# First experts and edge windows stepped beside the attention's node tiles

## The chip, the cores and the metric

The kernel runs on one core of one Trainium2 chip. The metric is the device time of one execution in microseconds (us): the median of three timed runs, and beside them one execution recorded by the hardware profiler. An execution with the profiler on can take longer than a timed one; the table below has both.

Engines in the profile: PE is TensorE's matmul, PEld its weight load, DVE is VectorE, ACT is ScalarE, POOL is GpSimd, SP is SyncE, which here only issues DMAs.

## The reference

The reference is four layers over a graph of 3125 nodes with 256 features and 53125 edges sorted by their destination. Each layer adds a graph step and a feed-forward step to `x`. Only the first two steps and the preparation of the later layers touch the change.

```python
def gnn0(x, bias, src, dst):             # attention over each node's incoming edges, 8 heads of 32
    h = layernorm(x)
    q, k, v = h @ Wq.T / SCALING, h @ Wk.T, h @ Wv.T
    attn = einsum('ehd,ehd->eh', k[src], q[dst]) + bias
    a = exp(attn - segment_max(attn, dst)[dst])
    a = a / segment_sum(a, dst)[dst]
    return segment_sum(v[src] * a[:, :, None], dst) @ Wo.T

def ffn0(x):                              # a shared network, and the best 2 of 4 small experts
    h = layernorm(x)
    shared = relu(relu(h @ sW1 + b) @ sW2 + b) @ sW3 + b        # 256 -> 256 -> 128 -> 256
    out[e] = relu(relu(h @ eW1[e] + b) @ eW2[e] + b) @ eW3[e]   # 256 -> 128 -> 64 -> 256
    topw = softmax(top_k(softmax(h @ gW + gb), 2))
    return shared + sum(topw * out[chosen])

x = x + gnn0(x); x = x + ffn0(x)          # then layers 1 to 3, whose graph steps sum the
                                          # features of each node's neighbours
```

## The kernel before

**Tiles and stages.** The nodes are 25 tiles of 125 (`T`, `P`), and `x` stays on the chip. `attention()` (L1526) is the first graph step; then `experts0` (L750) is the first feed-forward step, and beside it `blocks` (L1858) prepares for the later layers, whose neighbour sums are matmuls with blocks of counts: for each pair of node tiles, how many edges lead from each node of the one to each of the other. After both come `convolutions`, `experts1` and the rest.

**What sets the order.** A scheduling layer puts each engine's instructions in the order in which the Python code issues them and adds the waits. A tile taken from a pool waits until the last reader of the buffer has finished, so `bufs` says how far an engine may run ahead. Generators that one function runs with `next` place the work of another in between. The queues of SP and POOL issue DMAs in order.

**The attention's loop.** Its setup writes keys and values of all nodes to `kv_d` in DRAM, and finds `first`, the index of each node tile's first edge. Each tile has 18 columns of 128 edges (`WC`), in three parts of six (`PC`). Per tile, in the order of the loop at L1809:

- `logits` (three parts): POOL gathers six times 128 rows of `kv_d` (L1559, buffers `kv`, seven of them); PE multiplies a turned one-hot with the queries, held as three bf16 parts, into `qx` (L1738, three PSUM banks, a bank for two columns and six matmuls); DVE multiplies keys with it (L1741) and sums over each head (L1742).
- `sums_of`: adds the edges' bias, an Exp on ACT (L1751), and 18 matmuls that add up per node (L1754), read into `sums` (L1756).
- `weights_of`, for the tile before: 18 matmuls bring each node's shift back to its edges (L1766), DVE subtracts (L1767), ACT takes the Exp (L1771).
- `weighted`, for the tile before: DVE weighs the values (L1776), ACT casts the one-hot (L1781), and 18 matmuls in float32 of 265 columns collect `acc` (L1783, two PSUM banks).
- `one_hot`, `one_hot_turned`, `queries`, for the tile after: one-hots, 18 transposes (L1724), the loads `lt_t` (L1702) and `eb_t` (L1704) on SP, and the query product.
- `normed`, `normed_turned`, `projected`, for the tile before: division by the sum of weights, two transposes (L1800), the product with `wo`, and the addition to `x` (L1807). `normed` also writes the tile's in-degrees to `deg`.

The small products share the PSUM name `sm` (three banks).

**The first experts.** `experts0` goes by seven groups of four or three tiles (`GROUPS`), 500 or 375 columns, with pools of two buffers. A group is a layer norm (a Sqrt on ACT), eight transposes into `lt`, `gates` (some 25 small operations on DVE and an Exp on ACT), seven hidden products (`product` at L233, each followed by `relu_into`, which takes DVE at L745 and ACT at L747 in turn), the gates' spread over the experts (L809), and per tile a product `po` that is added to `x` (L817). Weights lie in one slot `wslot`, loaded by SP. After each of nine products a group calls `next(beside)`, one step of `blocks`.

**The count blocks.** `blocks` first finds, for each group of five nodes (`GN`; 25 groups to a tile, 625 in all), where its edges begin: prefix sums of `deg` as three matmuls and a scan, a store of `ptr_d` and a load of `win_at` on SP. Ten gathers on POOL (L1907) fetch the 128 edges from there on, sources and destinations; they are transposed (L1913) and turned by DVE operations on 625 columns into the row and tile of the source and the place of the destination (`row_h`, `til_h`, `col_h`). Then, for each of 25 destination tiles: three comparisons on DVE (L262: `hr`, `hc`, `hs`), 25 pairs of matmuls (L1960, L1962) whose results leave by DVE or ACT (L197, L199) as `ab`, 25 transposes (L1972) into `an`, and the stores of `ab` to `at_d` and of `an` to `an_d` (L105 and L106, two DMAs each on SP). From the third on, every second tile also issues one of ten clears of `xs_d`.

```python
attention()
with weights("main"):
    ...
        steps = blocks(bp, bps)
        experts0(steps)
        for _ in steps:
            pass
```

Of the kernel before, what the change touches and what calls it, by code (L numbers as in the profile page):

```python
# [26 lines left out]
E = 53125  # L27
# [14 lines left out]

GN = 5
# [25 lines left out]
def gnn_ffn_kernel(ctx: ExitStack, tc: tile.TileContext, a, out: bass.AP):  # L69
# [4 lines left out]
    wpools = []  # L74
# [42 lines left out]
    @contextmanager  # L117
    def weights(name):

        with tc.tile_pool(name="w" + name, bufs=2, reuse_waits="tile") as p:  # L120
            wpools.append(p)
            yield
            wpools.pop()

    def slot():
        return wpools[-1].tile([128, SLOT], F32, name="wslot", tag="wslot")
# [13 lines left out]
    def bias_rows(*names):  # L140


        v = wpools[-1].tile([3, ROWS], F32, name="wbias_in", tag="wbias_in", bufs=1)
        h = wpools[-1].tile([3, ROWS], BF16, name="wbias_h", tag="wbias_h", bufs=1)
        t = wpools[-1].tile([3, ROWS], BF16, name="wbias", tag="wbias")
# [20 lines left out]
    class Packer:  # L166
# [5 lines left out]
        def put(self, ap, rows_, shape):  # L172
            n = 1
            for s in shape:
                n *= s
            v = self.t[:rows_, self.at:self.at + n]
            if len(shape) == 2:
                v = v.rearrange("p (a b) -> p a b", a=shape[0])
            elif len(shape) == 3:
                v = v.rearrange("p (a b c) -> p a b c", a=shape[0], b=shape[1])  # L180
            nc.sync.dma_start(v, ap)
            self.at += n
            assert self.at <= SLOT
            return v
# [565 lines left out]
    def experts0(beside=iter(())):  # L750
# [17 lines left out]
        with ExitStack() as es:  # L768
            pool = es.enter_context(tc.tile_pool(name="ex0", bufs=2, reuse_waits="tile"))
            psum = es.enter_context(tc.tile_pool(name="ps_ex0", bufs=2, space=PSUM, reuse_waits="tile"))  # L770

            pick = pool.tile([4, 2, 128], F32, name="pick", bufs=1)
            nc.vector.tensor_copy(pick.rearrange("e p (j c) -> e (p j) c", j=2),
                                  ident[:4, :4].unsqueeze(2).to_broadcast([4, 4, 64]))
            for t0, n in GROUPS:
                ln = pool.tile([P, 4, D], F32, name="ln")
                normalize(pool, ln, x[:, t0:t0 + n, :], n, "a")
                lt = pool.tile([128, 2, 4, P], F32, name="lt")
                transposed(psum, lt, ln, n)
                g = gates(pool, psum, lt, n, gw, gb, 4, "softmax")  # L780
                gt = turned_gates(pool, psum, g, n, 4)
                c = n * P

                def hidden(name, m, terms, bias):
                    ps = psum.tile([128, 512], F32, name="tr")
                    product(ps[:m, :c], terms)
                    relu_into(name, ps[:m, :c], bias)
                    next(beside, None)

                s1 = pool.tile([128, 2, 4 * P], F32, name="s1")  # L790
                s2 = pool.tile([128, 4 * P], F32, name="s2")
                for m in range(2):
                    hidden(s1[:, m, :c], 128, [(sw1[:, k, m * 128:(m + 1) * 128], fan(lt[:, k, :n, :]))
                                               for k in range(2)], cols[:, m:m + 1])
                hidden(s2[:, :c], 128, [(sw2[:, k, :], s1[:, k, :c]) for k in range(2)], cols[:, 2:3])

                e2 = pool.tile([128, 2, 4 * P], F32, name="e2")
                for p in range(2):
                    ps2 = psum.tile([128, 512], F32, name="pair", bufs=1)
                    for j in range(2):  # L800
                        e = 2 * p + j
                        e1 = pool.tile([128, 4 * P], F32, name="e1")
                        hidden(e1[:, :c], 128, [(ew1[:, e, k, :], fan(lt[:, k, :n, :])) for k in range(2)],
                               cols[:, 3 + e:4 + e])
                        product(ps2[j * 64:(j + 1) * 64, :c], [(ew2[:, e, :], e1[:, :c])])
                    relu_into(e2[:, p, :c], ps2[:, :c], cols2[:, p:p + 1])
                    ps = psum.tile([128, 512], F32, name="tr")
                    product(ps[:, :c], [(pick[:, p, :], fan(gt[:, :n, :]))])
                    nc.vector.tensor_mul(e2[:, p, :c], e2[:, p, :c], ps[:, :c])  # L809
                    next(beside, None)  # L810
                for i in range(n):
                    at = slice(i * P, (i + 1) * P)
                    xt = x[:, t0 + i, :]
                    po = psum.tile([P, D], F32, name="po")
                    product(po, [(s2[:, at], sw3), (gt[:, i, :], eb3)]
                            + [(e2[:, p, at], ew3[:, p, :]) for p in range(2)], sb3)
                    nc.vector.tensor_add(xt, xt, po)  # L817
# [708 lines left out]
    def attention():  # L1526
# [10 lines left out]
        with ExitStack() as es:  # L1537
# [50 lines left out]
            first = pool.tile([1, T + 1], F32, name="first", bufs=1)  # L1588
            at = pool.tile([WB, 5], I32, name="win_at", bufs=1)

            def begins():
# [16 lines left out]
                nc.vector.tensor_scalar(first, first, float(E - WE), None, ALU.min)  # L1608
# [3 lines left out]
                nc.vector.tensor_tensor(win, first[:, :T].unsqueeze(2).to_broadcast([1, T, WC]),  # L1612
# [77 lines left out]
            psum = es.enter_context(tc.tile_pool(name="ps_att", bufs=3, space=PSUM, reuse_waits="tile"))  # L1690

# [37 lines left out]
            def logits(s, p):  # L1729
# [4 lines left out]
                for c0 in range(0, PC, 2):  # L1734
                    ps = psum.tile([128, 2, D], F32, name="qx")
# [37 lines left out]
            def weighted(s):  # L1773
                s.acc = psum.tile([P, 512], F32, name="acc", bufs=2)
# [36 lines left out]
            queries(now)  # L1811
            for t in range(T + 1):
                if now:
                    logits(now, 0)
                if before:
                    weights_of(before)
                    weighted(before)
                after = one_hot(t + 1) if t + 1 < T else None
                if before:
                    normed(before)  # L1820
                if after:
                    one_hot_turned(after)
                    queries(after)
                if now:
                    logits(now, 1)
                if before:
                    normed_turned(before)
                if now:
                    logits(now, 2)
                if before:  # L1830
                    projected(before)
                if now:
                    sums_of(now)
                before, now = now, after
# [23 lines left out]
    def blocks(pool, psum):  # L1858

        ptr_d = dram.tile([G], I32, name="ptr_d")  # L1860
        iota_h = pool.tile([128, HC], BF16, name="iota_h", bufs=1)
        nc.vector.tensor_copy(iota_h, iota[:, :HC])

        upto = pool.tile([P, GT], F32, name="upto", bufs=1)
        within = pool.tile([P, GT], F32, name="within", bufs=1)
        gn = pool.tile([P, GT + 1], F32, name="gn", bufs=1)
        nc.vector.tensor_scalar(gn, iota[:P, :GT + 1], float(GN), None, ALU.mult)
# [461 lines left out]
```

## Time and profile before

| what | value |
|---|---|
| timed runs, median | 3668.42 us (3662.62 to 3675.12) |
| the profiled execution's own time | 3862.84 us |
| its span | 3861.0 us |
| mean granted PE clock | 0.891 |
| PE busy | 3383.0 us, 88% |
| DVE busy | 1731.8 us, 45% |
| ACT busy | 1028.9 us, 27% |
| POOL busy | 614.6 us, 16% |

The times in views of the profile are those of the profiled execution and add up to its span; differences of timed runs are read against the median. A view of groups has a line of the code, the engine, the operation, output and inputs with their shapes, the count, then busy time, the mean in ns, and the idle time ahead of it. A line of waits has the waiting engine and instruction, what released it, and us in total, how often, and the longest. A line of the timeline has the start, the duration, and the instruction. In the busy tenths, the span is cut into 40 equal slices, and each digit is the busy share of a slice in tenths; PEclk is the granted clock in tenths of full speed.

### The profile page before, as it was taken

How to read it: one execution, taken by the hardware profiler on the slowest of the kernel's cores; microseconds unless marked ns; L12 is line 12 of the kernel's file. 1: busy time of each engine (PE TensorE's matmuls, PEld its weight loads, DVE VectorE, ACT ScalarE, POOL GpSimd, SP SyncE). 2: the span in 40 equal slices, each digit the busy share in tenths (PEclk: the TensorE clock that was granted, in tenths of full speed). 3: DMA queues.
4: the chain of work that ended last, by engine and by line, in shares of the span. 5: the costliest groups of instructions: out<-in, count | busy, mean ns of one | idle time of the engine just before them, and what ended most of it. 6: DMA issues, size and time to landing. Idle time of an engine off the chain costs nothing.

```text
span 3861.0 us, 45135 instructions
## 1 busy us (share of the span) xinstructions
PE 3383.0 (88%) x16645; PEld 2518.1 (65%) x16645; DVE 1731.8 (45%) x4687; ACT 1028.9 (27%) x1931; POOL 614.6 (16%) x588
## 2 busy tenths in 40 slices
PE   6577667777689889999999969997999999999998
PEld 3455555555366557888978758886875555568765
DVE  6466555555666565232346621114551111254561
ACT  1122112112123224232333212223432332332120
POOL 1545454444100000000001222220000000000000
PEclk9678777767769888999999879998989999999998
DMA  5645454444135544343433356665420000033101
GB/s 170 184 132 157 132 154 137 133 140 134 45 127 193 177 166 120 95 104 99 112 83 97 94 158 180 176 187 132 110 61 17 9 17 9 14 81 97 34 1 35
DMA packets 265708, 415.30 MB, mean 108 GB/s; under 512 B 40861, under 2 KB 206274, under 8 KB 265474
## 3 DMA queue, kind: packets, MB, share of 16 engines
q1 hardware_dynamic: 200242, 261.56, 23.1%
q0 software_dynamic: 51568, 134.33, 12.9%
q10 hardware_dynamic: 13663, 16.39, 1.6%
q8 instruction: 135, 2.21, 0.2%
q14 instruction: 100, 0.81, 0.1%
HBM read 313.72 MB, written 98.40 MB: 107 GB/s over the span
## 4 chain that ended last, share of the span: by engine, by line
PE 62%; DVE 2%; DMA 2%; ACT 1%; issue 0%; POOL 0%; SPq 0%; DVEq 0%; POOLq 0%; ACTq 0%
PE po L233 19%; PE agg L2063 18%; PE hid_ps L233 13%; PE tr L233 2%; PE row L233 1%; PE tok L1436 1%; PE po L231 1%; PE tr L223 1%; DMA x_d<-ys,to 1%; PE tr L2137 1%; PE bk L1972 1%; PE bk L1960 0%; ACT h L1277 0%; PE bdeg L1962 0%; PE s L233 0%
## 5 line engine op out<-in xcount | busy, mean ns | idle before, releaser
L2063 PE MATMUL agg<-cnt_f,hp 125*128 125x500 f32 (+1 forms) x3500 | 735.8, 370 | 24.0 <-ACT hp L2004 24.0
L2063 PEld LDWEIGHTS agg<-cnt_f,hp 125*128 125x128 f32 x3500 | 639.7, 190 | 108.7 <-ACT hp L2004 25.3
L1559 POOL DMA_INDIRECT kv<-kv_d,src_w x450 | 442.7, 984 | 419.1 <-PE acc L1783 200.2
L1738 PE MATMUL qx<-q_t,oht 125*128 125x256 bf16 x1350 | 266.2, 359 | 154.7 <-DVE kv L1741 94.7
L2041 ACT CAST cnt_f<-blk 125x500 fp32r<-125x500 bf16 (+1 forms) x435 | 245.8, 566 | 481.2 <-PE agg L2063 465.0
L2041 DVE CAST cnt_f<-blk 125x500 fp32r<-125x500 bf16 (+1 forms) x440 | 185.3, 422 | 294.9 <-PE agg L2063 249.7
L1738 PEld LDWEIGHTS <-oht 125*128 125x128 bf16 x1350 | 164.8, 125 | 233.9 <-issue 176.5
L1283 DVE SCALAR_TENSOR_TENSOR x<-po,gall,x 125x256 f32<-125x256 f32 x200 | 93.8, 483 | 417.9 <-PE po L233 417.4
L1277 ACT ACTIVATE h<-hid_ps,shift,scale 128x500 f32<-128x500 f32 (+1 forms) x224 | 161.9, 723 | 377.6 <-PE hid_ps L233 377.0
L1783 PE MATMUL acc<-kv,oh_f 128*125 128x265 f32 x900 | 237.0, 428 | 14.4 <-DVE kv L1776 14.4
L1783 PEld LDWEIGHTS acc<-kv,oh_f 128*125 128x125 f32 x900 | 187.9, 212 | 62.0 <-DVE kv L1776 22.2
L1741 DVE TENSOR_TENSOR kv<-kv,qx 128x512 f32<-128x512 f32 x225 | 149.9, 683 | 138.7 <-PE qx L1738 75.2
L233 PE MATMUL hid_ps<-xe,wslot 128*128 128x256 f32 x832 | 194.8, 387 | 11.4 <-DVE xe L1122 11.2
L233 PE MATMUL po<-wslot,h 128*125 128x256 f32 x800 | 203.0, 386 | 0.1
L233 PE MATMUL hid_ps<-h,wslot 128*128 128x500 f32 (+1 forms) x448 | 193.8, 556 | 4.1 <-ACT h L1277 0.6
L233 PEld LDWEIGHTS po<-wslot,h 128*125 128x125 f32 x800 | 145.0, 187 | 75.2 <-ACT h L1277 27.0
L233 PE MATMUL hid_ps<-v_rows,wslot 128*128 128x500 f32 (+1 forms) x448 | 187.2, 538 | 0.0
L233 PE MATMUL po<-wslot,hid 128*128 128x256 f32 x832 | 183.8, 379 | 0.0
L233 PEld LDWEIGHTS hid_ps<-xe,wslot 128*128 128x128 f32 x832 | 148.8, 191 | 44.7 <-DVE xe L1122 14.5
L997 POOL DMA_INDIRECT xs_d<-r_l,pos x50 | 59.5, 1191 | 722.9 <-DVE r_l L993 598.9
L233 PEld LDWEIGHTS po<-wslot,hid 128*128 128x128 f32 x832 | 158.1, 190 | 21.5
L1129 ACT ACTIVATE hid<-hid_ps,wslot 128x256 f32<-128x256 f32 x208 | 97.0, 474 | 279.7 <-PE hid_ps L233 279.7
(480 smaller groups left out, 4651.5 us busy)
## 6 DMA issues: line engine op xcount, KB each, us to landing
wslot<-in_ex_W SPq DMA_DIRECT2D x52, 1024.0 KB
blk<-an_d SPq DMA_DIRECT2D x60, 546.9 KB
xs_d<-nothing SPq DMA_DIRECT2D x10, 2730.0 KB
blk<-at_d SPq DMA_DIRECT2D x40, 546.9 KB
blk<-an_d SPq DMA_DIRECT2D x45, 410.2 KB
at_d<-ab SPq DMA_DIRECT2D x25, 683.6 KB
an_d<-an SPq DMA_DIRECT2D x25, 683.6 KB
blk<-at_d SPq DMA_DIRECT2D x30, 410.2 KB
```

The costliest lines, as they stand in the source:

```text
L223: nc.tensor.transpose(ps[:, i * P:(i + 1) * P], src[:, i, k * 128:(k + 1) * 128], ident[:P, :P])
L233: nc.tensor.matmul(ps, l, r, start=(bias is None and i == 0), stop=(i == last))
L997: st = nc.gpsimd.indirect_dma_start(out=xs_d, in_=l2[:, i, :], in_offset=None, out_offset=bass.IndirectOffsetOnAxis(ap=self.pos[s][:, t0 + ...
L1129: nc.scalar.activation(hid[:, m, :], ps[:, :BLK], AF.Gelu, bias=c[:, 4 + m:5 + m])
L1277: nc.scalar.activation(dst[:, m, :c], ps[:, :c], AF.Relu, bias=shift[:, l, col:col + 1], scale=scale[:, l, col:col + 1])
L1283: nc.vector.scalar_tensor_tensor(x[:, t0 + i, :], po, gating.all[:, t0 + i, e:e + 1], x[:, t0 + i, :], ALU.mult, ALU.add)
L1559: got = nc.gpsimd.indirect_dma_start(out=kv[:, c, KO:], out_offset=None, in_=kv_d, in_offset=bass.IndirectOffsetOnAxis(ap=src_i[:, at + c: ...
L1738: nc.tensor.matmul(ps[:, c, :], s.oht[:, p * PC + c0 + c, :], s.q[:, k, :], start=(k == 0), stop=(k == 2))
L1741: nc.vector.tensor_mul(k_, k_, ps)
L1783: nc.tensor.matmul(s.acc[:, :D + H + 1], of[:, c, :], kv[:, c, AO:VO], start=(p == 0 and c == 0), stop=(p == 2 and c == PC - 1))
L2041: to(f[:, :n, :], part[0][:, :n, m % MB, :])
L2063: nc.tensor.matmul(ps[f][:, :c], hp[:, m, k, f * 128:(f + 1) * 128], got[:, :c], start=(m == 0 and k == 0), stop=(m == T - 1 and k == 1))
```

## The change

The first experts go by pairs of node tiles, as steps that the attention's loop calls up to eight times per node tile. A pair may start when both its tiles have left the attention. The edges of the groups of five nodes are found for five node tiles at a time, in five steps each, one step per node tile of the attention from the fifth on; the gathers, transposes and operations are those of `blocks` before, on 125 columns at a time (quotient, then eleven operations into `self.row`, `self.tile` and `self.column`); where a tile's edges begin comes from `first`, which the setup already had. `blocks` keeps the count blocks alone. Beside it stand the steps of experts and windows that are left. In PSUM, `qx` goes from three banks to two and `acc` from two to one; the experts get one bank `tr` and one `pair`. Their pools (one buffer each) and their weights' slot are on another side of the memory until the blocks are done. The path for other inputs, not run here, keeps the experts by four.

```diff
-            first = pool.tile([1, T + 1], F32, name="first", bufs=1)
+            first = big.tile([1, T + 1], F32, name="first")
...
             psum = es.enter_context(tc.tile_pool(name="ps_att", bufs=3, space=PSUM, reuse_waits="tile"))
+            windows.begin(first, lambda: psum.tile([128, 512], F32, name="sm"))
...
-                    ps = psum.tile([128, 2, D], F32, name="qx")
+                    ps = psum.tile([128, 2, D], F32, name="qx", bufs=2)
...
-                s.acc = psum.tile([P, 512], F32, name="acc", bufs=2)
+                s.acc = psum.tile([P, 512], F32, name="acc", bufs=1)
...
+            more = experts()
             for t in range(T + 1):
+                def beside():
+                    more.step(t - 1)
+
                 if now:
                     logits(now, 0)
+                beside()
                 if before:
                     weights_of(before)
+                    beside()
                     weighted(before)
+                beside()
                 after = one_hot(t + 1) if t + 1 < T else None
                 if before:
                     normed(before)
                 if after:
                     one_hot_turned(after)
                     queries(after)
+                beside()
                 if now:
                     logits(now, 1)
+                beside()
                 if before:
                     normed_turned(before)
+                beside()
                 if now:
                     logits(now, 2)
                 if before:
                     projected(before)
+                beside()
                 if now:
                     sums_of(now)
+                beside()
+                if t >= Windows.TB:
+                    windows.next()
                 before, now = now, after
...
+    class Experts0:
+        def __init__(self, pools):
+            pool = pools.enter_context(tc.tile_pool(name="ex0_b", bufs=1, side="right", reuse_waits="tile"))
+            psum = pools.enter_context(tc.tile_pool(name="ps_ex0_b", bufs=1, space=PSUM, side="right",
+                                                    reuse_waits="tile"))
+            wpool = pools.enter_context(tc.tile_pool(name="w0", bufs=1, side="right", reuse_waits="tile"))
+            with weights_of_pool(wpool, (SLOT0, D)):
+                self.group = experts0_by(pool, psum, 2)
+            self.now, self.left = iter(()), [(t0, min(2, T - t0)) for t0 in range(0, T, 2)]
+
+        def step(self, ready):
+            for _ in self.now:
+                return True
+            if self.left and sum(self.left[0]) <= ready:
+                self.now = self.group(*self.left.pop(0))
+                return self.step(ready)
+            return False
+
+    def experts0_by(pool, psum, most):
...
+        def group(t0, n):
             ln = pool.tile([P, most, D], F32, name="ln")
             normalize(pool, ln, x[:, t0:t0 + n, :], n, "a")
+            yield
             lt = pool.tile([128, 2, most, P], F32, name="lt")
             transposed(psum, lt, ln, n)
+            yield
             g = gates(pool, psum, lt, n, gw, gb, 4, "softmax")
+            yield
             gt = turned_gates(pool, psum, g, n, 4)
...
+    class Windows:
+        TB = 5
...
+        def all(self, first):
...
+            for t0 in range(0, T, n):
+                ptr_d = dram.tile([P], I32, name=f"ptr{t0}_d")
+                some = deg[:, t0:t0 + n]
+                ps = self.ps()
+                nc.tensor.matmul(ps[:GT, 0:n], upto, some, start=True, stop=False)
+                nc.tensor.matmul(ps[:GT, 0:n], ones[0:1, :GT], starts[:, t0:t0 + n], start=False, stop=True)
+                nc.tensor.matmul(ps[:GT, 128:128 + n], within, some, start=True, stop=True)
+                ptr = pool.tile([GT, n], I32, name="ptr", bufs=1)
+                nc.vector.tensor_scalar(ptr, ps[:GT, 0:n], float(E - 128), None, ALU.min)
...
+                nc.sync.dma_start(ptr_d.rearrange("(t g) -> g t", g=GT), ptr)
+                at = pool.tile([P, 1], I32, name="win_p", bufs=1)
+                nc.sync.dma_start(at, ptr_d.rearrange("(q o) -> q o", o=1))
...
+                yield
+                got = []
+                for k in ("src", "dst"):
+                    w = pool.tile([P, 128], I32, name="win_" + k, bufs=1)
+                    nc.gpsimd.indirect_dma_start(
...
+                til, row, off, base = (small(v) for v in ("til", "row", "off", "base"))
+                quotient(til, row, src_f, small("qi", I32), off)
+                yield
...
+                yield
...
-    def blocks(pool, psum):
+    def blocks(pool, psum, windows):
...
+        windows.ps = lambda: psum.tile([128, 512], F32, name="bk")
...
+        row_h, til_h, col_h = windows.row, windows.tile, windows.column
...
         for t in range(T):
+            windows.next()
             hr, hc, hs = hot("hr", row_h, t, HC), hot("hc", col_h, t, HC), hot("hs", til_h, t, T + 1)
...
-    attention()
+    windows_pool = ExitStack()
+    windows = Windows(lambda: windows_pool.enter_context(
+        tc.tile_pool(name="windows", bufs=1, side="right", reuse_waits="tile")))
...
+    attention(windows, experts)
...
-            steps = blocks(bp, bps)
-            experts0(steps)
+            steps = blocks(bp, bps, windows)
             for _ in steps:
+                for _ in range(4):
+                    beside[0].step(T)
+            while beside[0].step(T):
                 pass
+        windows_pool.close()
```

## The prediction

> **What bounds the kernel now.** I read the busy tenths first, then the stages' windows, the groups, the waits, and last the timeline of single instructions.
>
> ```profile
> PE   6577667777689889999999969997999999999998
> DVE  6466555555666565232346621114551111254561
> PEclk9678777767769888999999879998989999999998
> ```
>
> A slice is 96.5 us. From slice 11 on PE is at 8 to 9 tenths: what is put there lengthens the kernel. Slices 1 to 10, the attention's loop, are the only long stretch with PE at 5 to 8 tenths and a clock of 7 or so. The change moves work from slices 10 to 15 into it. The stages' windows (microseconds; then busy time of PE, weight loads, DVE, ACT, POOL; the PE clock; the DMA share):
>
> ```profile
> 160.00:951.00 791.00, 567.61 (x3447) 428.19 (x3446) 460.52 (x724) 150.84 (x294) 397.20 (x403) 0.76 0.49 139
> 951.00:1003.00 52.00, 36.07 (x218) 27.33 (x217) 31.49 (x70) 9.34 (x20) 6.31 (x7) 0.84 0.17 49
> 1003.00:1079.00 76.00, 45.13 (x172) 25.64 (x173) 55.32 (x162) 11.19 (x19) 14.07 (x10) 0.66 0.21 50
> 1079.00:1442.00 363.00, 325.90 (x2310) 226.05 (x2308) 224.51 (x444) 108.81 (x182) 0.00 (x0) 0.83 0.50 170
> ```
>
> To 1003 it is attention: PE busy 0.72 at clock 0.76, so 0.545 of a full-clock PE. Then the stage of experts and count blocks to 1464.5, where the next layer begins: 461.5 us, most of it with PE 0.90 busy at 0.83, or 0.745.
>
> ```profile
> L1807 DVE TENSOR_TENSOR x<-x,sm x25: 406/414/422, 183.2 to 999.4; 125x256 f32<-125x256 f32 x25
> ```
>
> This line ends a node tile: (999.4 - 183.2)/24 = 34.0 us per tile. Its waits:
>
> ```profile
> POOL kv L1559 <- PE acc L1783: 200.2, 20, 12.7
> PE qx L1738 <- DVE kv L1741: 87.5, 42, 7.6
> DVE kv L1741 <- PE qx L1738: 68.6, 36, 4.3
> DVE sums L1756 <- remote: 56.9, 12, 6.5
> DVE l L1767 <- remote: 44.7, 11, 5.8
> ```
>
> POOL's 18 gathers take about 24 us of the 34, then wait until acc's matmuls free a buffer. DVE is 0.58 busy. PE and DVE wait for each other in turn: the loop is an in-order chain with slack on every engine, not one bound. "Remote" waits, whose releaser the profile doesn't show, sum to 132 us and occur only before 1003. The profiled execution took 3862.8 us (span 3861.0), the timed median is 3668.4: 194 less. I therefore put an estimated 150 of the 194 into the loop: timed period 34.0 - 150/25 = 28.0, with ends 34.0 (nothing there) and 26.2 (all of it).
>
> **What the Trainium skill says.** "TensorE: Matmul & The Clock Gate", Part 1: the clock is either half or full, full after about 3.4 us of steady work. The trace agrees in kind: stages average 0.66 to 0.84, the dense mixed one 0.83. So more PE work in the loop may buy clock. The same page, "Architectural detail": PE pulls only weight loads ahead, ACT and DVE are strictly first in, first out; the reciprocal waits of L1738 and L1741 agree. So an inserted step delays what stands behind it. "PSUM — Partial Sum Buffer", Specifications: eight banks. Before uses 3 sm + 3 qx + 2 acc, after 3 + 2 + 1 and two for the experts; both fill it. "ScalarE: Activation LUTs", What ACT_TABLE_LOAD costs: about 1283 ns, and a drain; this trace's loads are 1283 ns.
>
> **Part 1, what leaves the stage.** In the instruction order of the changed kernel eleven groups of two tiles, and the first eight of group 11's fourteen steps, stand between the attention's matmuls; the last six and group 12 (one tile) remain, beside the first five blocks: about 1.86 of 25 tiles. All edge windows but four of the 25 steps move as well. The stage becomes a short head, 25 blocks and this tail.
>
> A block: DVE's three comparisons and five or six evacuations shared with ACT.
>
> ```profile
> L262 DVE TENSOR_TENSOR hr<-iota_h,row_h 128x3150 bf16<-128x3150 bf16 x25 | 44.7, 1790 | 0.1
> L262 DVE TENSOR_TENSOR hc<-iota_h,col_h 128x3150 bf16<-128x3150 bf16 x25 | 44.6, 1789 | 0.0
> L262 DVE TENSOR_TENSOR hs<-iota_h,til_h 128x650 bf16<-128x650 bf16 x25 | 12.3, 492 | 4.0 <-PE bdeg L1962 3.8
> ```
>
> 1.79 + 1.79 + 0.49 + 5.5 x 0.68 = 7.8 us of DVE; PE has 75 matmuls at about 0.058 us, 4.4 us at full clock and 8 at half. So 8 to 9.4. The 24 intervals between at_d stores average 15.8 with experts between; the one where a block is almost alone:
>
> ```profile
> 1449.61 0.30 SPq L105 DMA_DIRECT2D at_d<-ab  x1
> ...
> 1459.03 0.30 SPq L105 DMA_DIRECT2D at_d<-ab  x1
> ```
>
> 9.4 us. I take 9.0. Stores and clears need at most 9 us of transfers per block (two of 3.06 each, a clear of 7.3 every second block), so they hide, just. Head: before, the first at_d store came 75.8 us after attention, with 29.3 us of POOL waiting for win_at; after, two to_row, comparisons and a first block, 12 us. End: 5.5 us from the last store to the next layer. Tail: 1.86 x 6.8 (below) = 12.6. New stage: 12 + 24 x 9.0 + 5.5 + 12.6 = 246. Saved: 461.5 - 246 = 215.
>
> **Part 2, what enters the loop.** PE at full clock: a product in float32 is two passes. A 500-column pass starts every 0.42 us:
>
> ```profile
> 1031.20 0.19 PEld L233 LDWEIGHTS tr<-lt,wslot 128*128 128x128 f32 x1 [0.23 <-issue]
> 1031.62 0.19 PEld L233 LDWEIGHTS tr<-lt,wslot 128*128 128x128 f32 x1 [0.23 <-issue]
> ```
>
> 40 such passes per four tiles give 4.2 us per tile (250 columns halve the pass and double the count); eight output passes of 256 columns at 0.216 give 1.7; gates, transposes and bias, counted at the same prices, 0.9. Sum 6.8. The attention's own work per tile: 54 qx at 0.11 = 5.9, 36 acc passes of 265 columns at 0.224 = 8.1, 54 short ones 2.8, eight projections at 0.216 = 1.7, the rest 0.4: 18.9, or 0.556 of 34.0, which checks the 0.545 above. Together 25.7.
>
> DVE: 5.35 us per tile (per pair 4.0 in small gate operations, 2.2 in relus, 2.8 in normalising, 1.7 in products and sums), since gates are paid 13 times instead of 7; windows add 24 small operations per five tiles, 1.1 per tile. DVE's 19.8 (460.5/791 x 34.0) becomes 26: still under the period I reach. ACT: a Sqrt and an Exp load per pair, 2.6 us per two tiles; ACT waits 303.9 us in the loop for the weights, which covers it; uncovered, in front of the Exp of L1771 that gates acc, 1.3 per tile. POOL: two window gathers per five tiles queue ahead of kv gathers, 0.6 per tile, inside POOL's 7 to 9 us waits; uncovered, 0.6. SP: a ptr store, a waiting win_p load and twelve weight loads once stand ahead of lt_t and eb_t loads, which already wait for buffers; uncovered, a few us in total.
>
> The banks: PE may run two qx groups ahead of DVE, not three, and acc's next tile waits until normed has read it. Before shows no such row, so bounds: nothing (DVE reads qx at once) to 3 us per tile (one group of six matmuls plus a multiply, 0.66 + 0.68, twice). Inside the coupling I take none on top of the efficiency below.
>
> At what efficiency does PE work with two streams? The mixed stage reached 0.745. I take 0.74: 25.7/0.74 = 34.7, against 28.0. That is 6.7 more, on the 23 tiles that carry the load: +154.
>
> **Sum.** 154 - 215 = -61. Against the profiled execution's own time that is 3863 - 61 = 3802, if its period grew alike; for timed runs 3668.4 - 60.9 = **3608**. Zero gain lies at 215/23 = 9.3 us per tile.
>
> **Rivals.** *Hidden better.* If the surplus isn't in the loop (period 34.0 timed too), 25.7 at 0.70 is 36.7: +2.7 x 23 = 62, gain 153, time 3515. For it: PE idle 28% and POOL's waits; against it: the 132 us of remote waits. With everything hidden, 3453.
> *Slower by the in-order chain.* Every step stalls the chain whole: 6.8/0.76 = 8.9 us of PE, plus 1.6 of DVE work in the chain (an evacuation that waits for its product blocks the multiplies behind it): 10.5 x 23 = 241, +26, time 3694. It decides beyond 9.3 us. For it: PE and DVE already wait for each other, one tr bank serialises product and relu, and qx has a bank less; against it: PE has idle time with nothing ready.
> *Blocks alone don't shrink.* Many at_d intervals before are 11 to 13; at 12.5, 24 x 3.5 = 84 comes back: 3692. For it: half-clock PE and handovers through two banks; against it: 9.4, 9.5 and 9.4 occur.
> *The change doesn't do what it says*: the instruction order excludes it.
>
> **How the numbers follow.** Main 0.47, own range 3560 to 3655; hidden better 0.20; chain 0.20; blocks 0.13. Low 3490 leaves out about 0.08 below, high 3715 about 0.1 above; in these lie the base's two ends. What a measurement can tell here is about 0.3%, 11 us. Faster: 0.20 + 0.45 of the main + 0.03 of the blocks' case = 0.68. Same: 0.02 + 0.04 + 0.04 = 0.10. The rest, 0.22, slower.
>
> **What would show it.** Spacing of L1807's counterpart in the loop 34 to 36 in timed terms, near 38 to 40 profiled, PE there over 0.85 busy at a clock above 0.76; at_d stores 9 to 9.5 apart after the first five; stage near 246. If the row of PE qx waiting for DVE grows beyond 200 us and remote waits stay, the chain rival holds; if the spacing stays at 34 to 36, hidden better; at_d at 12 means the blocks'. Wrong altogether if the surplus is spread evenly or if ACT's table loads end the chain's waits.

## The result, and the profile after

The changed kernel takes 3656.73 us (median of 20 runs, 3647.29 to 3667.49) against 3668.07 for the kernel before (20 runs, 3658.96 to 3675.12): ratio 0.9972, 95% interval 0.9963 to 0.9982, or 11 us faster. In a later series (`a_again`) it was 0.9969 (0.9955 to 0.9983). I had predicted 3608, 60 us faster: the sign is right, the size is not, and a fifth of the gain arrived.

The busy tenths of the kernel after (slices of 91.5 us):

```profile
PE   6699989899788799999999699979999999999998
DVE  6577777777676632323456311135631111344561
PEclk9799989989755699999988799989989999999898
```

Slices 3 to 10, the loop, are now at 8 to 9 on PE with the clock at 8 to 9: the experts fill them. But slices 12 and 13, in the count blocks, show 8 on PE at a clock of 5. The stages' windows of the kernel after (us; busy PE, weight loads, DVE, ACT, POOL; clock; DMA share), the loop, the head, the blocks with the experts' tail, the blocks alone:

```profile
160.00:947.00 787.00, 717.51 (x4498) 535.70 (x4496) 592.83 (x1362) 217.57 (x435) 442.45 (x421) 0.92 0.52 145
947.00:968.00 21.00, 10.67 (x64) 9.00 (x64) 13.55 (x38) 5.80 (x10) 2.43 (x2) 0.52 0.43 109
968.00:1048.00 80.00, 68.41 (x584) 57.49 (x584) 59.83 (x128) 27.24 (x47) 0.00 (x0) 0.78 0.47 153
1048.00:1248.00 200.00, 158.60 (x1327) 147.94 (x1328) 137.02 (x213) 65.93 (x104) 0.00 (x0) 0.50 0.80 268
```

The line that ends a node tile, in the kernel after:

```profile
L1856 DVE TENSOR_TENSOR x<-x,sm x25: 403/412/422, 171.4 to 946.6; 125x256 f32<-125x256 f32 x25
```

(946.6 - 171.4)/24 = 32.3 us per tile. The loop's main waits after:

```profile
POOL kv L1607 <- PE acc L1832: 95.9, 18, 14.2
DVE kv L1790 <- PE qx L1787: 23.3, 31, 2.3
PE qx L1787 <- DVE kv L1790: 19.1, 18, 1.6
```

PE waits less for DVE than before (19 us against 60 in `b_again`, a second recording of the kernel before, below) although it has a qx bank less: the experts' matmuls now stand in these gaps.

This profile spans 3659.5, about its timed runs. In the first recording of the kernel before (3861), and in the two of the six series below in which this kernel took about 3800, the attention's loop of every kernel was 3 to 7 us per tile slower, with "remote" waits and for a reason that no run shows, and loops are compared only in the other recordings.

### The profile page after: what moved, and what is told of

Its sections match the earlier page's. It is cut to its first block, busy times and chain, and to the rows that moved or that the text cites. A ratio compares the mean times of both kernels' runs of the same rounds, so it can differ in the third digit from the quotient of the medians.

```text
span 3659.5 us, 46125 instructions
## 1 busy us (share of the span) xinstructions
PE 3369.1 (92%) x16909; PEld 2563.3 (70%) x16909; DVE 1756.6 (48%) x4982; ACT 1056.6 (29%) x2003; POOL 638.3 (17%) x587
## 4 chain that ended last, share of the span: by engine, by line
PE 78%; DVE 9%; DMA 7%; issue 3%; ACT 2%; POOL 1%; SPq 0%; ACTq 0%; DVEq 0%; POOLq 0%
PE agg L2144 20%; PE po L242 20%; PE hid_ps L242 14%; PE acc L1832 5%; DMA kv<-kv_d,src_w 4%; PE tr L242 3%; PE qx L1787 2%; PE bk L2053 2%; PE row L242 2%; PE bdeg L2043 1%; PE bk L2041 1%; DVE kv L1790 1%; PE tok L1484 1%; DVE kv L1825 1%; PE tr L232 1%
## 5 line engine op out<-in xcount | busy, mean ns | idle before, releaser
L2144 PE MATMUL agg<-cnt_f,hp 125*128 125x500 f32 (+1 forms) x3500 | 738.0, 371 | 24.4 <-ACT hp L2085 24.4
L1607 POOL DMA_INDIRECT kv<-kv_d,src_w x450 | 465.1, 1034 | 303.0 <-PE acc L1832 95.9
L1787 PE MATMUL qx<-q_t,oht 125*128 125x256 bf16 x1350 | 217.8, 301 | 43.6 <-DVE kv L1790 33.8
L1832 PE MATMUL acc<-kv,oh_f 128*125 128x265 f32 x900 | 234.8, 426 | 11.6 <-DVE kv L1825 11.5
L242 PE MATMUL hid_ps<-xe,wslot 128*128 128x256 f32 x832 | 194.9, 387 | 10.6 <-DVE xe L1170 10.4
L1787 PEld LDWEIGHTS <-oht 125*128 125x128 bf16 x1350 | 139.1, 107 | 90.2 <-issue 43.8
L242 PEld LDWEIGHTS po<-wslot,h 128*125 128x125 f32 x800 | 145.0, 187 | 75.2 <-ACT h L1325 27.2
L1790 DVE TENSOR_TENSOR kv<-kv,qx 128x512 f32<-128x512 f32 x225 | 151.1, 681 | 37.1 <-PE qx L1787 24.4
```

What stands on the lines that cost most here:

```text
L242: nc.tensor.matmul(ps, l, r, start=(bias is None and i == 0), stop=(i == last))
L1607: got = nc.gpsimd.indirect_dma_start(out=kv[:, c, KO:], out_offset=None, in_=kv_d, in_offset=bass.IndirectOffsetOnAxis(ap=src_i[:, at + c: ...
L1787: nc.tensor.matmul(ps[:, c, :], s.oht[:, p * PC + c0 + c, :], s.q[:, k, :], start=(k == 0), stop=(k == 2))
L1790: nc.vector.tensor_mul(k_, k_, ps)
L1832: nc.tensor.matmul(s.acc[:, :D + H + 1], of[:, c, :], kv[:, c, AO:VO], start=(p == 0 and c == 0), stop=(p == 2 and c == PC - 1))
L2144: nc.tensor.matmul(ps[f][:, :c], hp[:, m, k, f * 128:(f + 1) * 128], got[:, :c], start=(m == 0 and k == 0), stop=(m == T - 1 and k == 1))
```

## The experiments

### The kernel before, again, and its banks

`b_again` is the kernel before, unedited.

> The kernel before, recorded once more, to learn the attention's period without the 194 us that its first recording had on top. If all of them lay in the loop, as the changed kernel's stages suggest (its profile is 3659.5, and its time up to the first agg matmul 1291.6), a recording near 3668 shows x additions 26 us apart and the stage of experts and blocks at 455 to 465 us. If they were spread over the kernel, the period is near 30 and the later stages are shorter than in the first recording.

Measured: 3681.57, span 3679.5. Its tile line:

```profile
L1807 DVE TENSOR_TENSOR x<-x,sm x25: 408/419/422, 169.8 to 816.4; 125x256 f32<-125x256 f32 x25
```

(816.4 - 169.8)/24 = 26.9 us per tile, with the at_d stores from 897.1 to 1273.8. So nearly all of the 194 us had been in the loop, and the timed base is 26.9, not my 28.0. Two of its waits in this loop:

```profile
POOL kv L1559 <- DMA kv<-kv_d,src_w: 73.6, 125, 2.2
POOL kv L1559 <- PE acc L1783: 4.6, 12, 1.2
```

POOL hardly waits for acc here (200 us in the first recording). It gathers for 437 of 646 us and waits another 74 until earlier gathers have landed, and DVE waits longer for gathered rows (77.7 us) than for the query product (29.3). So the loop at 26.9 us per tile ran close to the pace of its gathers; the slack that I had read on POOL was that of the first recording. In the changed kernel POOL waits for acc again (95.9 us above), and PE is 0.91 busy.

`b_banks`:

```diff
-                    ps = psum.tile([128, 2, D], F32, name="qx")
+                    ps = psum.tile([128, 2, D], F32, name="qx", bufs=2)
...
-                s.acc = psum.tile([P, 512], F32, name="acc", bufs=2)
+                s.acc = psum.tile([P, 512], F32, name="acc", bufs=1)
```

> The kernel before with two qx banks and one acc bank, nothing else. If the banks cost nothing beyond what I took (none), 3665 to 3672. If the loop needs them, up to 3 us per tile: 3668 + 75 = 3743 at the upper bound, with more PE qx waiting for DVE. If the rival of the in-order chain is right it is at least 20 us slower.

Measured: 1.0011 (1.0003 to 1.0019), a loop of 27.2 us per tile. The banks cost at most 0.3 us per tile; I had taken nothing for them.

### Filler matmuls, and half of the experts left in place

`a_warm`:

```diff
+        warm = psum.tile([128, 512], F32, name="warm", bufs=1)
...
+                nc.tensor.matmul(warm, ident_h, hr.rearrange("p g c -> p (g c)")[:, :512], start=True, stop=True)
                 evacuate(ab[:, :, g0:g0 + n, :],
```

> The changed kernel with one dense bf16 matmul of 512 columns, into a bank that nobody reads, after each four groups of a count block: seven per block, 1.5 us of PE at full clock and 3.0 at half. Theory clock: the blocks alone run at half clock because their short matmuls leave the array idle too often; dense work lifts the clock, blocks go from 10.6 us to 8.5 to 9.5, DVE's 7.8 bounds them, and the kernel gets 20 to 50 us faster than the changed one (3605 to 3637). Theory stores: the two stores and clears bind (DMA share 0.83), so nothing is gained, 3655 to 3670. Theory chain at fixed clock: 2 to 3 us per block more, 3700 to 3730.

Measured: 0.9972 (0.9959 to 0.9985), as without them. The fillers lifted the clock, to 0.80 on average from 1060 to 1180. Windows of `a_warm`, of which the second covers two and a half blocks at full clock:

```profile
1112.00:1124.00 12.00, 9.62 (x85) 7.74 (x83) 6.80 (x9) 4.37 (x6) 0.00 (x0) 0.72 1.02 348
1124.00:1148.00 24.00, 17.02 (x219) 14.23 (x220) 19.23 (x22) 8.41 (x13) 0.00 (x0) 1.00 0.85 284
```

The spacings of at_d there are 9.6 and 9.0, against about 12 where the clock is lower, and 11.0 on average over sixteen blocks from the seventh on (10.6 without the fillers). The time is the one that the theory of the stores had named. But blocks are shorter where the clock is full, and the fillers' own cost isn't known apart, so the theory of the clock was neither shown nor refuted.

`a_split`:

```diff
+                calls = []
+
                 def beside():
-                    more.step(t - 1)
+                    calls.append(t)
+                    if len(calls) % 2:
+                        more.step(t - 1)
```

> The changed kernel with every second call of an experts' step in the attention left out, so that half of the groups stay for the count blocks (four steps per block, as the changed kernel has there already). Theory clock: the loop's period falls by about 3 us (24 x 3 = 72), and the blocks, with dense products beside them, take about 12 us each instead of 11.65 on average, so that little of it comes back: 3570 to 3610. Theory stores or chain: the blocks take 10.6 + 3.4/0.75 = 15 us while experts last (22 of 25), +85, so 3650 to 3690.

Measured: 1.0042 (1.0016 to 1.0068), 25 us slower than the changed kernel. The loop gained what was expected (29.1 us per tile, 3.2 less), but the stores went from 885.7 to 1272.0: 386 us in place of 280, so the time lies where the second theory had put it. Experts by pairs beside the blocks cost more than in the loop. Why wasn't tried: single buffers and the single `tr` bank could explain it.

### Each part alone

`w_only` and `w_only2` are one kernel, the windows' part alone:

```diff
-            more = experts()
...
-                    more.step(t - 1)
+                    pass
...
-                    ps = psum.tile([128, 2, D], F32, name="qx", bufs=2)
+                    ps = psum.tile([128, 2, D], F32, name="qx")
...
+                for k, _ in enumerate(group(*at)):
+                    if 3 <= k < 12:
+                        next(beside, None)
...
             steps = blocks(bp, bps, windows)
+            experts0(steps)
             for _ in steps:
-                for _ in range(4):
-                    beside[0].step(T)
+                pass
```

with two acc banks again. `e_only` and `e_only2` are the experts' part alone:

```diff
-                if t >= Windows.TB:
-                    windows.next()
...
+        for _ in range(T):
+            windows.next()
         row_h, til_h, col_h = windows.row, windows.tile, windows.column
...
         for t in range(T):
-            windows.next()
```

`a_noexp` and `a_noexp2` leave the experts out, so that the later layers work on other values:

```diff
         def step(self, ready):
+            return False
```

> The windows' part alone: their steps stand beside the attention's tiles as in the changed kernel, but the experts go by four beside the count blocks as in the kernel before, with three qx and two acc banks. Theory A (the gain is the windows' head, the experts' move gives nothing): the stage after attention loses some 54 us of head less about 20 us in which experts ran there, the loop pays at most 1.5 us per tile: 3630 to 3660, at or below the changed kernel. Theory B (my prediction's: moving experts pays, since the blocks alone are short): it is slower than the changed kernel by the experts' gain, above 3665.

> The experts' part alone: the experts by pairs stand beside the attention as in the changed kernel, but all 25 steps of the windows are made ahead of the first count block. Theory A: the loop keeps most of its 5.4 us per tile more, and the stage's head is long again, now with little beside it (25 steps, five rounds through DRAM, some 60 to 80 us): 3700 to 3730, slower than before. Theory B: the windows cost little where they are, 3665 to 3680.

> The changed kernel with the first experts left out altogether (their weights are still loaded), so the loop carries the windows alone and the count blocks have nothing beside them from the first to the last. It prices both: if the loop's 5.4 us per tile are the experts', its period falls back to 27 to 28 us, else (banks, windows) it stays above 29. The blocks: 10.5 us each from the second on and a clock of 0.50 throughout if the blocks' price is their own at half clock; about 9.0, as I predicted, if the experts' tail or their buffers slowed them. Time about 3656 - 5 x 24 - 17 = 3520.

Measured, in a series whose kernel before took 3798.5: `w_only` 0.9977 (0.9954 to 1.0001), `e_only` 1.022 (1.0187 to 1.0254), `a_noexp` 3741.4, with loops of 31.1, 39.0 and 33.1 us per tile. Of this only the blocks are used: in `a_noexp` they took 10.0 and 11.1 in turn, as beside the experts' tail. All were therefore run again:

> The changed kernel once more, on the chip that runs the two parts below, so that all three are compared on one chip: 0.995 to 0.999 of the kernel before. In the series before this one the attention's loop was slow for every kernel (31 to 39 us per tile), and the kernel before stood at 3798.5; if that happens here too, this run shows what the change is worth there.

> The windows' part alone again, beside the changed kernel. Theory A (all of the gain is the head that the windows leave; the experts' move costs the loop what it saves the stage): at or below the changed kernel, 0.985 to 0.997 of the kernel before. Theory B (the experts' move pays): above the changed kernel, 0.998 or more.

> The experts' part alone again, beside the changed kernel. Theory A: 1.012 to 1.025 of the kernel before, since the head is long and has nothing beside it. Theory B: 0.998 to 1.003.

> The changed kernel without the first experts (left out; their weights are still loaded), beside the changed kernel on one chip: the difference of the two loops is the price of the experts in the loop, 4 to 5.4 us per tile, and the difference of the two stages is the price of their tail, 12 to 18 us. The count blocks alone took 10.55 us each, at a clock of 0.5, in the series before; the same here.

Measured: `a_again` 0.9969 (0.9955 to 0.9983), `w_only2` 1.0066 (1.0044 to 1.0089), `e_only2` 1.0069 (1.0051 to 1.0087), `a_noexp2` 3617.0. Each part alone makes the kernel slower by 0.7%; together they make it faster. Theory A falls with `w_only2`; theory B, which named its time, falls with `e_only2`, which lies between the two. The casts of hp, whose last one ends the first convolution, show it; one line each of `b_again`, `w_only2`, `e_only2` and `a_again` (start of the first and last cast at the end):

```profile
L2004 ACT CAST hp<-v x75: 388/405/409, 1288.7 to 1754.8; 125x256 fp32r<-125x256 f32 x75
```

```profile
L2085 ACT CAST hp<-v x75: 394/405/409, 1304.9 to 1773.0; 125x256 fp32r<-125x256 f32 x75
```

```profile
L2084 ACT CAST hp<-v x75: 399/407/417, 1320.1 to 1763.1; 125x256 fp32r<-125x256 f32 x75
```

```profile
L2085 ACT CAST hp<-v x75: 399/406/418, 1283.3 to 1726.3; 125x256 fp32r<-125x256 f32 x75
```

| us | loop ends | per tile | from there to the last hp | last hp |
|---|---|---|---|---|
| before (`b_again`) | 816.4 | 26.9 | 938.4 | 1754.8 |
| windows moved (`w_only2`) | 839.6 | 28.1 | 933.4 | 1773.0 |
| experts moved (`e_only2`) | 930.2 | 31.7 | 832.9 | 1763.1 |
| both (`a_again`) | 946.3 | 32.3 | 780.0 | 1726.3 |
| both, experts left out (`a_noexp2`) | 844.0 | 28.1 | 778.5 | 1622.5 |

All but `b_again` are of one series on one chip.

With the experts in their old place, moving the windows shortens the rest by 5 us and the loop pays 23. The blocks begin 56 us earlier after the loop, but the experts' last addition comes later. `w_only2` and `b_again`:

```profile
L863 DVE TENSOR_TENSOR x<-x,tr x25: 409/421/423, 951.6 to 1301.2; 125x256 f32<-125x256 f32 x25
```

```profile
L817 DVE TENSOR_TENSOR x<-x,po x25: 410/421/423, 917.9 to 1256.1; 125x256 f32<-125x256 f32 x25
```

That is 461.6 and 439.7 us after the loop: as these lines read, the stage is held by the sum of experts and blocks, and its long head was the experts' time. With the experts gone the head stands bare. `e_only2`, from the loop's end to the first store:

```profile
930.00:1020.00 90.00, 48.47 (x184) 29.47 (x182) 50.90 (x202) 10.41 (x18) 14.51 (x10) 0.50 0.17 32
```

90 us with PE half busy at half clock. Then moving the windows is worth 832.9 - 780.0 = 53 us for 16 in the loop. `a_noexp2` gives the prices: 32.3 - 28.1 = 4.3 us per tile for the experts in the loop, 1.1 for the windows without the experts (also 28.1 in `w_only2`, with the old banks), and 1.5 us for the tail. Beside the experts the windows add 32.3 - 31.7 = 0.7. The whole time of `a_noexp2` is no price: behind the last hp its later layers took longer, and of the 104 us that it is ahead there 41 are left at the end.

### What sets a block's price

> The changed kernel with the bdeg matmuls of all but the first node tile left out (24 x 25 short matmuls; the out-degrees are then wrong). If the block is bound by PE at half clock, the 25 matmuls cost their 2.8 us and the block falls from 10.55 to 8 to 9.4: then the interval of 9.4 from which I priced it was short because it held none of them. If DVE or the stores bind, it stays at 10 or more.

`a_nodeg` leaves out the bdeg matmuls of all but the first tile, so that the out-degrees are wrong and only the blocks are used:

```diff
-                    nc.tensor.matmul(ps_n, hr[:, g, :P], hs[:, g, :T], start=(t == 0 and g == 0),
-                                     stop=(t == T - 1 and g == GT - 1))
+                    if t == 0:
+                        nc.tensor.matmul(ps_n, hr[:, g, :P], hs[:, g, :T], start=(g == 0), stop=(g == GT - 1))
```

> The changed kernel with four PSUM banks for the products of a count block in place of two. In the steady stretch PE idles some 1.9 of 10.55 us per block, waiting for evacuations. If the handover sets the price, blocks fall to 8.7 to 9.5 us and the kernel gains 20 to 45 us on the changed one; if the clock or the stores (DMA share 0.83) set it, they stay above 10 and the kernel within 10 us.

`a_bk4` has four banks for `bk`, here and in the other places that ask for it, `a_bk4warm` these and the fillers of `a_warm`:

```diff
-                ps = psum.tile([128, 512], F32, name="bk")
+                ps = psum.tile([128, 512], F32, name="bk", bufs=4)
```

> Four banks and the seven filler matmuls of 512 columns per block. With the clock at full, PE's own work is 4.4 + 1.5 us, below DVE's 7.8. If the half clock sets the price, blocks fall below those with four banks alone, to 8 to 9.5 us. If blocks don't fall though the clock is lifted, something else bounds them: DVE's order of comparisons and evacuations, or the stores (two of 3.06 and half a clear of 7.3 us: 9.8).

Measured: `a_nodeg` 3665.5, with blocks of 9.7 and 8.9 in turn; `a_bk4` 0.988 (0.9824 to 0.9937); `a_bk4warm` 0.9889 (0.9857 to 0.9922). The steady stretch in the windows from 1060 to 1180 of `a_again`, `a_nodeg`, `a_bk4`, `a_bk4warm`:

```profile
1060.00:1180.00 120.00, 101.30 (x856) 94.83 (x855) 81.63 (x100) 40.52 (x62) 0.00 (x0) 0.50 0.84 280
```

```profile
1060.00:1180.00 120.00, 80.54 (x617) 71.55 (x616) 86.55 (x105) 44.09 (x69) 0.00 (x0) 0.50 0.90 299
```

```profile
1060.00:1180.00 120.00, 83.91 (x916) 80.43 (x915) 86.37 (x113) 41.47 (x67) 0.00 (x0) 0.65 0.87 287
```

```profile
1060.00:1180.00 120.00, 86.36 (x987) 74.58 (x986) 89.13 (x115) 41.16 (x66) 0.00 (x0) 0.84 0.83 278
```

PE 0.84 busy at half clock (first) is near its bound; the bdeg matmuls are 1.2 us of a block of 10.6 (10.0 and 11.1 in turn). With four banks, `a_bk4` waits elsewhere in the same stretch:

```profile
ACT ab L208 <- DMA at_d<-ab: 26.6, 4, 8.4
DVE ab L206 <- DMA at_d<-ab: 17.0, 3, 6.4
```

The stores are what is late next: sixteen steady blocks still take 10.8 us each, and 10.6 with the fillers, whether the clock is 0.65 or 0.84. The kernel nevertheless gained, 277 to 266 us over all blocks, 6.5 in the head and 4 behind the last store. Of what was expected of `a_bk4` each case came half true: the blocks stayed above 10, the kernel gained more than 10. The kernel before has no such banks to give: its experts ask for five and its blocks for three, all eight. `a_early` and `a_bk4early` issue the clears in the loop:

```diff
+            clear = clear_slots(windows.pool)
...
                 if t >= Windows.TB:
                     windows.next()
+                    if t % 2:
+                        next(clear, None)
...
-            if t > 2 and t % 2 == 0:
-                next(clear, None)
```

(the experts' slot is 3089 wide here, for room).

> The changed kernel with the ten clears of xs_d issued in the attention's loop (every second tile from the fifth on) in place of every second count block. If the two banks and the half clock set the block's price, the blocks stay at 10 us or more (at most the 1.1 us by which every second one is longer goes), and the loop may pay some us: 0.993 to 1.001 of the kernel before. If the stores and clears set it, they fall to 9 or less: 0.985 to 0.992.

> The same with four banks. If stores and clears bound the blocks of a_bk4, these fall from 10.7 to 8 to 9 us, DVE's 7.8 being next: 0.975 to 0.985 of the kernel before. If they stay above 10, it is DVE and ACT's order, and the time is that of a_bk4, 0.988.

> Four banks and the clears in the attention's loop, once more. In the series before, the stretch of the blocks was 225 us in place of 277, and the loop was slow for every kernel. With the loop at its usual speed: the changed kernel's 0.997 less 52 us of blocks, plus 0 to 10 us in the loop and its start: 0.982 to 0.986 of the kernel before; 0.988 to 0.990 if the clears cost the start and the loop more than that.

Measured: `a_early` 1.0053 (1.0034 to 1.0072) and `a_bk4early` 0.9894 (0.987 to 0.9919), in a series whose kernel before took 3819.4; `a_bk4early2` 0.9896 (0.9879 to 0.9912) in one with 3675.8. With two banks the blocks stay at 11.1 to 11.2 without any clear among them, DMA share 0.46, so the clears didn't set the price there: PE's work at half clock and its handovers through two banks did. (The blocks of 10.0, every second one with the clears, are gone; PE's order of bdeg matmuls and transposes differs between the two runs, and no run tried it alone.) With four banks and no clears the same sixteen blocks fall to 8.7 us, as expected, but the time doesn't. Windows of `a_bk4early`, the second and third without experts:

```profile
1146.00:1220.00 74.00, 65.49 (x609) 57.47 (x609) 59.66 (x128) 30.14 (x52) 0.00 (x0) 0.78 0.46 145
1220.00:1300.00 80.00, 66.05 (x620) 62.47 (x619) 65.80 (x87) 26.37 (x42) 0.00 (x0) 0.58 0.48 151
1300.00:1372.00 72.00, 53.83 (x690) 49.95 (x689) 68.43 (x125) 34.29 (x57) 0.00 (x0) 0.86 0.65 208
```

Blocks are 10.1 where the clock is low and 6.8 where it is up, with DVE 0.95 busy; whether the clock made them short or short blocks lifted the clock wasn't tried. All blocks take 230 us in `a_bk4early2`, but its clears start at 128 us and cost the setup 13 us and the loop 1.4 per tile (33.7), so the time is that of `a_bk4`. Four banks alone, one argument of the tile `bk`, is the shortest edit among those at 0.988 to 0.990; it was timed beside the kernel before, not beside the changed one.

## Why the prediction was wrong in size

By its own steps, from `b_again` and `a_again`:

| step | predicted | measured |
|---|---|---|
| period before, timed | 28.0 | 26.9 |
| period after | 34.7 | 32.3 |
| cost in the loop | +154 | 946.3 - 816.4 = +130 |
| head, to the first at_d store | 12 | 23.8 |
| 24 blocks and tail | 216 + 12.6 | 277.4 |
| saved after the loop, to the last hp | 215 | 158 |
| sum | -61 | -28 |

**The loop** was right in mechanism and put 24 us too dear. The work by count, 25.7 us at full clock, got through in 32.3, an efficiency of 0.80 and not 0.74: the clock rose from 0.88 to 0.92. Banks cost at most 0.3, windows 0.7 to 1.1, experts 4.3; the table loads were not tried apart. The sign rests on this error: with +154 in the loop the 158 us saved would have left 4.

**The step that failed is the block's price, "I take 9.0".** I had read it from an interval of 9.4 at the end of the stage and called it a block almost alone. The groups of the kernel before in that interval:

```profile
L1960 PE MATMUL bk<-hc,hr 128*125 128x125 bf16 x25 | 3.8, 300 | 1.8 <-ACT ab L199 0.7 <-DVE ab L197 0.5 <-DVE an L197 0.3
L1972 PE MATMUL bk<-ident_h,ab 125*125 125x125 bf16 x25 | 3.1, 313 | 0.8 <-DVE ab L197 0.6 <-ACT an L199 0.3
```

It holds 50 of a block's 75 matmuls; the 25 bdeg ones had come earlier, and so had DVE's three comparisons, 4.1 us by my own prices, of which it holds none. In `a_again` the steady stretch from 1060 to 1180 has all three:

```profile
L2041 PE MATMUL bk<-hc,hr 128*125 128x125 bf16 x275 | 38.3, 305 | 13.0 <-ACT ab L208 6.0 <-DVE ab L206 3.4 <-ACT an L208 2.7
L2053 PE MATMUL bk<-ident_h,ab 125*125 125x125 bf16 x282 | 35.5, 316 | 5.7 <-DVE ab L206 5.7
L2043 PE MATMUL bdeg<-hs,hr 128*125 128x25 bf16 x299 | 34.0, 260 | 0.0
```

I had written 8 us of PE at half clock for all 75, which was near (a run of 25 bdeg takes 2.8, and PE is busy for 8.9 us per block), and then let the short interval outvote it and added no idle for the handovers, PE's waits until DVE or ACT has read a bank: the gaps ahead of bk are 18.7 us over these 11 blocks, 1.7 each. Measured 10.6 over sixteen steady blocks, 26 us more than 16 x 9.0. Without the bdeg matmuls (`a_nodeg`) a block takes 9.7 and 8.9 in turn, about the price that I had read without them. What I had named as the rival of the blocks that don't shrink was right in kind (half clock, two banks), at 10.6 where I had put 12.5. My sum for stores and clears was short as well: 3.06 twice and half of 7.3 are 9.8 where every second block has a clear, above the 9.0 that they were to hide under; it cost nothing until four banks had taken the other limit away.

The other misses are of the same stage. The head is 24 us, with PE half busy (at a clock of 0.52 in the window of the result), +12. I had given nothing to the last round of the windows, which stands in it: in `a_again` the last `ptr` is stored at 946.9, its gathers are issued at 960.0, and DVE stands still until they have landed:

```profile
964.13 0.23 DVE L1985 CAST win_f<-win_src 125x128 f32<-125x128 int32 x1 [5.85 <-DMA win_src<-in_src,win_p]
```

The first six blocks took 77.6 in place of 66.6. Without the experts' tail (`a_noexp2`) they take 77.2; with most of the windows' steps ahead of them, and a part of the tail beside them (`e_only2`), 65.0. That points to the windows' last steps once more, though no run moved these alone. The last two blocks took 29.5: the convolution's normalisation runs on DVE and ACT ahead of the evacuations, 11.5 more.

**From -28 to -11.** Later layers gave back 4 us in these two recordings (24.4 left at the very last hp cast). The rest is mostly spread of the executions: the recording of `b_again` lay 8.7 above its series' median and that of `a_again` 4.9 below its own.

**What held:** the sign and the whole range, 3490 to 3715; that the surplus lay in the loop; that PE clock would rise there; that the banks cost next to nothing. **What didn't:** the in-order chain (10.5 us per tile) and the loop's remote waits as its sign, which none of the other recordings has; and that POOL's waits cover the window gathers: the loop before hardly has such waits, and the windows cost 1.1 us per tile there, 0.7 where the experts bring the waits back.

The Trainium skill, "TensorE: Matmul & The Clock Gate", Part 1, has the clock rise after about 3.4 us of sustained activity. Here PE is 0.84 busy by the records from 1060 to 1180 of `a_again` and stays at 0.50, while the same short matmuls ran at 0.65 with four banks (PE 0.70 busy) and at 0.86 in the last window of `a_bk4early` (0.75 busy). So the busy share of the records alone doesn't tell whether the clock rises. The fillers lifted it; what else counts, no run here shows.

## What to carry to other kernels

Work that is hidden beside other work has a price only in pairs: ask what the stage that is left will have beside it, and at what clock. The experts cost 4.3 us per tile in the loop; what they left behind were blocks at half clock and, without the second part of the change, a bare head of 90 us. And before an interval is used as a price, count its instructions: one that lacks a third of them is no price.

## What the runs showed of the hardware

Three limits of a count block lie close together: PE at half clock with two banks (10.6 to 11.2 us, with clears beside it or not), stores and clears at a DMA share of 0.87 (10.8), and, once both are gone, something that goes with the clock (10.1 at a low one, 6.8 at a high one with DVE 0.95 busy). Filler matmuls lifted the clock from 0.50 to 0.80 with two banks and from 0.65 to 0.84 with four, and the kernel was no faster for either.
